# A pipelined Mamba block on one core: the order of the state sums, a one-tick shift of the post-processing, and the W2 additions on ScalarE and GpSimd

## The chip, the cores and the metric

The kernel runs on one core of one Trainium2 chip. The metric is device time in microseconds of one execution, as the median of several runs. The engines are named by short names: PE is TensorE (matmuls; PEld its weight loads), DVE is VectorE, ACT is ScalarE, POOL is GpSimd, SP is SyncE, which issues nearly all DMAs.

## The reference, cut to what matters

The input is x of shape (4, 1024, 256), float32, and all arithmetic is float32.

```
x = x + block(layernorm(x))
x = x + (fwht(silu(n @ W1.T) * (n @ W3.T))) @ W2.T      # n = layernorm(x), hidden 1024

block(h):                       # h is (4, 1024, 256)
  z, xs, B, C, raw = split(rmsnorm(h) @ in_proj.T)       # 256, 64, 64, 256, 128 columns
  dt = softplus(raw @ dt_proj.T + bias)                  # 256 channels, 32 states each
  for each time step:  s = exp(dt * A) * s + dt * xs * B ;  y = sum over states of s * C
  h = h + ((y + xs * D) * silu(z)) @ out_proj.T
  h = h + (silu(r @ gate.T) * (r @ up.T)) @ down.T       # r = rmsnorm(h), hidden 704
```

The recurrence over 1024 time steps has 256 channels x 32 states per batch element. The Hadamard transform (fwht) is folded into W2 at the start, into the tile `w2h`.

## The kernel before, in words

**Units and ticks.** The work is cut into 8 units: 4 batch elements times 2 halves of 512 time steps (`c` is 0 or 1; a unit with c = 1 starts from states that the unit before kept in `carry`). A unit's scan is 16 steps q, each with 4 tiles `da` of 128 x 512: 128 rows are 4 channels times 32 states, 512 columns are time. A step takes two ticks of the program, with two of the four tiles in each, so a unit's scan is 32 ticks, and E = 32k + 31 is the last tick of unit k.

**What a tick of the scan does.** ACT makes two exponentials (line 725) for the step after the present one, that is two ticks ahead. DVE makes one product `bx` of two tiles (line 749; it reads `ub` from a DMA and `pb`, the copy of B in PSUM that ACT makes once for eight steps, line 738) and two scans (line 759). POOL then multiplies two tiles of the tick before by C (line 777), keeps their last column in `carry` for c = 0 (line 776), or multiplies the first column of the next tick's tiles by it for c = 1 (`start_from`, line 766, which the next scans wait for). In every even tick PE sums the states of the step before with four matmuls (`sum_states`, line 791), each from one tile to 32 rows of one PSUM tile `py`. Tiles 0 and 1 are multiplied in the tick before, tiles 2 and 3 in the same tick. The sums free the `da` tile, of which there are 4, for a DMA three steps ahead. After eight steps DVE adds x * D (`y_dx`, line 806) one tick after the last sum and POOL multiplies by silu(z) (`y_z`, line 811) one tick after that.

**What runs around it.** The steps of `pre(u, H)` prepare unit u, whose scan begins at tick H: row statistics, `un`, transposes, the projections x and dt's input (`pe_x`, `act_x`), dt (`pe_dt`), C (`pe_c`). The steps of `post(u, E, other)` follow its scan, beside the scan of the next units: the out projection wo and its addition to `hr` (from E+3), row statistics, `small2` (rsqrt, on POOL), `hn`, its transposes and their copies `ht`, the gated product of the 704 hidden columns in two groups of three chunks (`gated`: gate projections pg on PE, then up projections pu, silu of pg on ACT, copies of pu on ACT, the product on POOL), `wd` and its addition, row statistics, `small3`, `hn`, transposes, the gated product with W1 and W3 in groups of 3, 3 and 2 chunks, then W2 with its addition from E+36 and the store at E+43. The last is at the time of the next unit's E+4 and after, so that one unit's W2 follows the next unit's wo on PE. `gated` also takes in the z projections of the unit after next (`other`), if there is one.

**What sets the order.** The order is written by hand. `at(tick, lane, fn)` puts a step on a tick and a lane. The main loop at the end (lines 853 to 891) runs over the ticks, and in each runs the lanes in a fixed order: PE, ACT, the `bx` product, ACTb (`pb` alone), two exponentials, first scan, the DVE lane, second scan, POOL0, the multiplication by C, `start_from`, POOL, the sums, PEend, ACTend, SP, the scan's DMAs, SPend. Steps of one lane and tick stand in the order in which they were put there: those of all `pre` first, then those of `post` from the earliest unit on. Every engine works off its instructions in the order of the program, so an engine that waits for one step holds up all behind it. `copy_b` (`pb`) is on the last lane but one before the exponentials, in the tick before each eighth step, that is at E+16 and E+32 of a unit's post-processing.

**PSUM and copies.** All matmuls but the sums write to `dense`, a ring of four PSUM tiles of 128 x 512; a new one waits until the one four before has been read. The copies `up` use a ring of three tiles in SBUF.

In `add_rows` (line 296) each of the four row tiles t takes one matmul per chunk, two row tiles share a PSUM tile, and DVE adds that to `hr` with one instruction of 128 x 512 (line 316) one tick after the second.

Of the kernel before, what the change touches and what calls it, by code (L numbers as in the profile page):

```python
# [9 lines left out]
F32 = mybir.dt.float32  # L10
AF = mybir.ActivationFunctionType
ALU = mybir.AluOpType
# [3 lines left out]
P = 128  # L16
# [3 lines left out]
T = 512  # L20
TT = T // P
# [6 lines left out]
def tile_block(ctx: ExitStack, tc: tile.TileContext, a, out):  # L28
# [20 lines left out]
    nc = tc.nc  # L49
# [112 lines left out]
    def row_stats(u, src, ts, centred=True):  # L162

        if 0 in ts:
            u["mv"] = sm.tile([P, 2, TT], F32, tag="mv", name="mv")
        for t in ts:
            junk = p1.tile([P, DM], F32, tag="junk", name="junk")
            nm, ms = u["mv"][:, 0, t : t + 1], u["mv"][:, 1, t : t + 1]
            if centred:
                nc.scalar.activation(  # L170
                    junk, src[:, t, :], AF.Identity, scale=-1.0 / (16 * DM), accum_out=nm
                )
            nc.scalar.activation(
                junk,
                src[:, t, :],
                AF.Square,
                bias=nm if centred else 0.0,
                scale=1.0 / 16,
                accum_out=ms,
            )  # L180
# [27 lines left out]
    def transposes(u, src):  # L208

        u["pt"] = [dense_psum() for _ in range(2)]  # L210
        for k in range(2):
            for t in range(TT):
                nc.tensor.transpose(  # L213
                    u["pt"][k][:, t * P : (t + 1) * P], src[:, t, k * P : (k + 1) * P], ident
                )
# [22 lines left out]
    def at(tick, lane, fn, *args):  # L238
        todo[tick][lane].append(partial(fn, *args))
# [5 lines left out]
    def gated(tick, u, dst, wa, wb, chunks, src, z=None):  # L245


        g = [{} for _ in chunks]
        pe_z, act_z = z[0]["z"] if z else (None, None)

        def pe(i, name, w):
            c, n = chunks[i]
            if n < P:

                both = project(W[w], c * P, 2 * n, u[src])
                g[i]["pg"], g[i]["pu"] = both, both[n:]
            else:
                g[i][name] = project(W[w], c * P, n, u[src])

        def silus():  # L260
            for i, (_, n) in enumerate(chunks):
                g[i]["si"] = p3.tile([P, T], F32, tag="si", name="si")
                nc.scalar.activation(g[i]["si"][:n], g[i]["pg"][:n], AF.Silu)  # L263
            if z:
                act_z(z[1])

        def up(i):
            n = chunks[i][1]
            g[i]["up"] = p3.tile([P, T], F32, tag="up", name="up")
            nc.scalar.copy(g[i]["up"][:n], g[i]["pu"][:n])  # L270

        def product(i):
            c, n = chunks[i]
            nc.gpsimd.tensor_tensor(u[dst][:n, c, :], g[i]["si"][:n], g[i]["up"][:n], ALU.mult)  # L274

        three = len(chunks) == 3
        steps = [(i, *s) for s in (("pg", wa), ("pu", wb)) for i in range(len(chunks))]
        steps = [s for s in steps if chunks[s[0]][1] == P or s[1] == "pg"]
        late = z and len(steps) == 6
        steps = [(pe, *s) for s in steps]  # L280
        if z:
            steps.insert(3, (pe_z, z[1]))
        for k, step in enumerate(steps):
            at(tick + k // 2, "PE", *step)
        at(tick + 1, "ACTend" if three else "ACT", silus)
        at(tick + 2, "ACT", up, 0)
        for i in range(1, len(chunks)):
            if i == 2 and late:
                at(tick + 3, "ACT", up, i)
            else:  # L290
                at(tick + 2, "ACTend", up, i)
        at(tick + 2, "POOL", product, 0)
        for i in range(1, len(chunks)):
            at(tick + 3, "POOL", product, i)

    def add_rows(tick, u, lhs, rhs, per_tick, lane="PE"):

        po = {}

        def pe(t):  # L300
            if t % 2 == 0:
                po[t // 2] = dense_psum().rearrange("p (t d) -> p t d", t=2)
            left, right = lhs(), rhs()
            n = len(left)
            for k in range(n):
                nc.tensor.matmul(  # L306
                    po[t // 2][:, t % 2, :],
                    lhsT=left[k][:, t * P : (t + 1) * P],
                    rhs=right[k],
                    start=(k == 0),  # L310
                    stop=(k == n - 1),
                )

        def add(i):
            hr = u["hr"][:, 2 * i : 2 * i + 2, :]
            nc.vector.tensor_tensor(hr, hr, po[i], ALU.add)  # L316

        for t in range(TT):
            at(tick + t // per_tick, lane, pe, t)
            if t % 2:  # L320
                at(tick + t // per_tick + 1, "DVE", add, t // 2)


    def pre(u, H):

        s = {}
# [217 lines left out]
        if H == 32:  # L544

            at(0, "ACTend", lambda: row_stats(u, u["x"], (0, 1)))
            at(1, "ACTend", lambda: row_stats(u, u["x"], (2, 3)))
            at(3, "POOL", small)
            at(5, "POOL", small_end)
            at(4, "ACT", un, (0, 1))  # L550
            at(5, "ACT", un, (2, 3))
            at(6, "PE", lambda: transposes(u, s["un"]))
            at(6, "ACTend", transposed, u, "ut")
        else:
            at(H - 54, "SP", load_x, u)
            at(H - 45, "ACTend", lambda: row_stats(u, u["x"], (0, 1)))
            at(H - 43, "ACTend", lambda: row_stats(u, u["x"], (2, 3)))
            at(H - 39, "POOL", small)
            at(H - 37, "POOL", small_end)
            at(H - 32, "ACT", un, (0, 1))  # L560
            at(H - 31, "ACT", un, (2, 3))
            at(H - 30, "PE", lambda: transposes(u, s["un"]))
            at(H - 30, "ACTend", transposed, u, "ut")
        at(H - 25, "PE", pe_x)
        at(H - 24, "ACT", act_x)
        at(H - 23, "SP", dma_xb)
        at(H - 19, "SPend", dma_xr, 0)
        at(H - 17, "SPend", dma_xr, 1)
        at(H - 16, "PE", pe_dt)
        at(H - 16, "PE", pe_c, 0)  # L570
        if H == 32:
            for h in range(2):
                at(H - 11, "PE", pe_z, h)
# [16 lines left out]
    def post(u, E, other):  # L590


        s = {}
# [41 lines left out]
            4,  # L635
            "PEend",
        )
        at(E + 5, "ACTend", lambda: row_stats(u, u["hr"], (0, 1), False))
        at(E + 6, "ACTend", lambda: row_stats(u, u["hr"], (2, 3), False))
        at(E + 7, "POOL", small2)  # L640
        at(E + 8, "ACT", hn, "r3", None)
        at(E + 9, "PE", lambda: transposes(u, s["tok"]))
        at(E + 9, "ACTend", transposed, u, "ht")
        at(E + 9, "POOL", lambda: nc.gpsimd.tensor_tensor(u["hr"], u["hr"], u["x"], ALU.add))
        at(E + 10, "PE", big, "m")
        sizes = [min(P, DFF - c * P) for c in range(6)]
        chunks = list(enumerate(sizes))
        for i in range(2):
            gated(E + 10 + 3 * i, u, "m", "wg", "wu", chunks[3 * i : 3 * i + 3], "ht",
                  (other, i) if other else None)  # L650
        add_rows(
            E + 18,
            u,
            lambda: [u["m"][:n, c, :] for c, n in enumerate(sizes)],
            lambda: [W["wd"][:n, c, :] for c, n in enumerate(sizes)],
            1,
        )
        at(E + 20, "ACTend", lambda: row_stats(u, u["hr"], (0, 1)))
        at(E + 22, "ACTend", lambda: row_stats(u, u["hr"], (2, 3)))
        at(E + 23, "POOL", small3)  # L660
        at(E + 24, "ACT", hn, "r4", "nm")
        at(E + 25, "PE", lambda: transposes(u, s["tok"]))
        at(E + 25, "ACTend", transposed, u, "xt")
        at(E + 26, "PE", big, "g")
        chunks8 = [(c, P) for c in range(8)]
        for i in range(3):
            gated(E + 26 + 3 * i, u, "g", "w1", "w3", chunks8[3 * i : 3 * i + 3], "xt")
        add_rows(
            E + 36,
            u,  # L670
            lambda: [u["g"][:, c, :] for c in range(8)],
            lambda: [w2h[:, c, :] for c in range(8)],
            1,
        )
        at(E + 43, "SPend", store)

# [107 lines left out]
    def sum_states(q):  # L784
        s = qs[q]
        u = s["u"]
        first, last = s["n"] % 8 == 0, s["n"] % 8 == 7
        if first:
            u["py"] = ps_y.tile([P, T], F32, tag="y", name="py")
        for b in range(4):  # L790
            nc.tensor.matmul(  # L791
                u["py"][32 * b : 32 * b + 32, :],
                lhsT=rsel[:, 2 * s["j"] + s["g"], :],
                rhs=s["da"][:, b, :],
                start=first,
                stop=last,
            )
        if last:
            at(2 * q + 3, "DVE", y_dx, u, s["h"])
            at(2 * q + 4, "POOL0", y_z, u, s["h"])  # L800
# [159 lines left out]
```

## Time and profile before

| | |
|---|---|
| median of 3 runs | 1186.88 us (1186.69 to 1189.98) |
| the profiled execution | 1190.86 us, span of its instructions 1189.1 us |
| granted TensorE clock, mean | 0.903 |
| PE busy | 1023.6 us, 86% of the span |
| DVE busy | 961.1 us, 81% |
| POOL busy | 903.0 us, 76% |
| ACT busy | 773.8 us, 65% |
| two scans (line 759), mean of one | 1210 ns, 512 of them |
| multiplication by C (line 777) | 2358 ns, 256 of them |
| product of silu and up (line 274) | 1272 ns, 64 with W1 and W3, 48 of the first gated product |
| addition to `hr` on DVE (line 316) | 675 ns, 48 of them |
| copy of a PSUM tile on ACT (line 270) | 578 ns |

A timeline row gives the start and the length in us, the engine, the line, the operation, the tiles written and read, how many instructions were merged, and in brackets the idle time of the engine before it with what ended it. A matmul of float32 leaves two records on PE, so "x8" at line 791 is the four sums of one step. Lengths of neighbouring instructions of an engine overlap a little, so the cost of one that stands between others is read from start to start.

### The profile page before, as it was taken

To read this page: it belongs to the slowest core of one execution; us is meant where nothing else is said; L and a number is where in the kernel's file an instruction comes from. 1 tells how busy PE (TensorE), PEld (TensorE's weight loads), DVE (VectorE), ACT (ScalarE), POOL (GpSimd) and SP (SyncE) were. 2 spreads that over 40 slices of the span, in tenths; PEclk is the share of its full clock that TensorE was granted. 3 is DMA by queue.
4 is the path that set the end of the run, shared out by engine and by line. 5 is a ranking of instruction groups with operands and counts; after the bars stand their busy time and mean duration, and the time that the engine had idled before them with its cause. 6 is when DMAs were issued, how large, how long until landed. Compare 5 with 4: busy or idle time off the path is not lost.

```text
span 1189.1 us, 12244 instructions
## 1 busy us (share of the span) xinstructions
PE 1023.6 (86%) x3374; PEld 471.1 (40%) x3374; DVE 961.1 (81%) x860; ACT 773.8 (65%) x1391; POOL 903.0 (76%) x807
## 2 busy tenths in 40 slices
PE   8475467989998989988998989988998989699988
PEld 3121022433633355433634354433634353336535
DVE  4797889899889979899889979898989989992000
ACT  3746564878478775879478767878576847573331
POOL 6675768879788978889788978889787978784212
PEclk9776668989898889989998989988998989889989
DMA  7989998898699879888799869998689869840000
GB/s 246 336 308 355 358 338 296 310 329 284 238 337 306 327 244 313 318 327 296 252 339 313 302 225 342 313 335 282 242 315 322 308 243 328 307 155 1 18 0 18
DMA packets 89444, 321.91 MB, mean 271 GB/s; under 512 B 9312, under 2 KB 20000, under 8 KB 73120
## 3 DMA queue, kind: packets, MB, share of 16 engines
q1 hardware_dynamic: 87520, 318.38, 75.7%
q10 hardware_dynamic: 1856, 2.75, 0.6%
q8 instruction: 27, 0.44, 0.1%
q14 instruction: 41, 0.34, 0.1%
HBM read 302.22 MB, written 18.87 MB: 270 GB/s over the span
## 4 chain that ended last, share of the span: by engine, by line
PE 44%; POOL 16%; DVE 10%; issue 8%; DMA 4%; ACT 4%; SPq 0%; DVEq 0%; POOLq 0%; ACTq 0%
PE dense L226 23%; PE dense L306 14%; POOL da L777 10%; PE py L791 6%; DVE da L759 5%; DVE bx L749 4%; POOL g L274 3%; ACT da L725 1%; DMA ub<-ud 1%; DMA cd<-cc 1%; POOL m L274 1%; DVE hr L316 1%; PE dense L213 1%; DMA xr<-xbd 1%; POOL yt L811 1%
## 5 line engine op out<-in xcount | busy, mean ns | idle before, releaser
L777 POOL TENSOR_TENSOR da<-da,cr 128x1024 f32<-128x1024 f32 x256 | 603.7, 2358 | 100.1 <-DVE da L759 52.2
L759 DVE TENSOR_TENSOR_SCAN da<-da,bx 128x512 f32<-128x512 f32 x512 | 602.0, 1210 | 43.7 <-ACT da L725 10.4
L725 ACT ACTIVATE da<-da,nega 128x512 f32<-128x512 f32 x508 | 331.4, 713 | 68.8 <-DMA da<-dtd 65.4
L791 PE MATMUL py<-da,rsel 128*32 128x512 f32 x1024 | 226.7, 685 | 134.7 <-POOL da L777 132.8
L749 DVE TENSOR_TENSOR bx<-ub,pb 128x1024 f32<-128x1024 f32 x254 | 312.1, 1229 | 30.5 <-ACT pb L738 19.2
L226 PE MATMUL dense<-xt,w 128*128 128x512 f32 x512 | 228.8, 601 | 0.0
L226 PEld LDWEIGHTS dense<-xt,w 128*128 128x128 f32 x512 | 95.6, 191 | 136.0 <-issue 111.8
L791 PEld LDWEIGHTS py<-da,rsel 128*32 128x32 f32 x1024 | 29.9, 113 | 270.7 <-POOL da L777 213.8
L316 DVE TENSOR_TENSOR hr<-hr,dense 128x512 f32<-128x512 f32 x48 | 32.4, 675 | 127.6 <-PE dense L306 127.6
L306 PE MATMUL dense<-w2h,g 128*128 128x256 f32 x512 | 113.4, 380 | 0.0
L306 PE MATMUL dense<-wd,m 128*128 128x256 f32 (+1 forms) x384 | 103.6, 417 | 0.9 <-POOL m L274 0.9
L306 PEld LDWEIGHTS dense<-w2h,g 128*128 128x128 f32 x512 | 96.8, 190 | 18.4 <-issue 5.5
L270 ACT COPY up<-dense 128x512 f32<-128x512 f32 x112 | 63.4, 578 | 58.3 <-PE dense L226 58.1
L274 POOL TENSOR_TENSOR g<-si,up 128x512 f32<-128x512 f32 x64 | 80.8, 1272 | 25.8 <-ACT up L270 25.4
L226 PE MATMUL dense<-ut,win 128*128 128x512 f32 x192 | 94.1, 623 | 0.2 <-ACT ut L220 0.2
L274 POOL TENSOR_TENSOR m<-si,up 128x512 f32<-128x512 f32 (+1 forms) x48 | 60.4, 1273 | 41.3 <-ACT up L270 41.3
L226 PE MATMUL dense<-ht,wg 128*128 128x512 f32 x192 | 89.4, 610 | 2.6 <-ACT ht L220 2.6
L263 ACT ACTIVATE si<-dense 128x512 f32<-128x512 f32 x112 | 63.0, 596 | 39.7 <-PE dense L226 38.1
L306 PEld LDWEIGHTS dense<-wd,m 128*128 128x128 f32 (+1 forms) x384 | 72.3, 201 | 40.0 <-issue 24.0
L200 ACT ACTIVATE hn<-hr,s 128x256 f32<-128x256 f32 x64 | 30.3, 543 | 88.9 <-POOL s L196 74.8
L226 PE MATMUL dense<-ht,wu 128*128 128x512 f32 x160 | 72.2, 597 | 0.0
L776 POOL COPY carry<-da 128x2 f32<-128x2 f32 x128 | 23.8, 186 | 61.5 <-DVE da L759 59.5
(92 smaller groups left out, 798.5 us busy)
## 6 DMA issues: line engine op xcount, KB each, us to landing
da<-dtd SPq DMA_DIRECT2D x127, 1024.0 KB
ub<-ud SPq DMA_DIRECT2D x254, 512.0 KB
cr<-cd SPq DMA_DIRECT2D x64, 256.0 KB
x<-in_x SPq DMA_DIRECT2D x8, 512.0 KB
dtd<-dt SPq DMA_DIRECT2D x16, 256.0 KB
ud<-du SPq DMA_DIRECT2D x16, 256.0 KB
cd<-cc SPq DMA_DIRECT2D x16, 256.0 KB
out<-hr SPq DMA_DIRECT2D x8, 512.0 KB
```

Of the source, the lines that this page charges most:

```text
L200: nc.scalar.activation(dst[:, t, :], src[:, t, :], AF.Identity, bias=bias[:, t : t + 1] if bias is not None else 0.0, scale=scale[:, t : t ...
L226: nc.tensor.matmul(dst[:n], lhsT=w[:, k, col : col + n], rhs=src[:, k, :], start=(k == 0), stop=(k == 1),)
L263: nc.scalar.activation(g[i]["si"][:n], g[i]["pg"][:n], AF.Silu)
L270: nc.scalar.copy(g[i]["up"][:n], g[i]["pu"][:n])
L274: nc.gpsimd.tensor_tensor(u[dst][:n, c, :], g[i]["si"][:n], g[i]["up"][:n], ALU.mult)
L306: nc.tensor.matmul(po[t // 2][:, t % 2, :], lhsT=left[k][:, t * P : (t + 1) * P], rhs=right[k], start=(k == 0), stop=(k == n - 1),)
L316: nc.vector.tensor_tensor(hr, hr, po[i], ALU.add)
L725: nc.scalar.activation(da, da if q else s["u"]["pdt", b], AF.Exp, scale=an[:, s["h"], s["j"], b, s["g"] : s["g"] + 1],)
L749: nc.vector.tensor_tensor(s["bx"], s["ub", b0 // 2], u["pb"].unsqueeze(1).broadcast_to([P, 2, T]), ALU.mult)
L759: nc.vector.tensor_tensor_scan(da, da, s["bx"][:, b % 2, :], start, ALU.mult, ALU.add)
L777: nc.gpsimd.tensor_tensor(s["da"][:, two, :], s["da"][:, two, :], s["cr"].unsqueeze(1).broadcast_to([P, 2, T]), ALU.mult,)
L791: nc.tensor.matmul(u["py"][32 * b : 32 * b + 32, :], lhsT=rsel[:, 2 * s["j"] + s["g"], :], rhs=s["da"][:, b, :], start=first, stop=last,)
```

## The change

The states of a step are summed beginning with tiles 2 and 3. In the post-processing the row statistics of the four row tiles behind wo are taken in one tick, and all steps from there to the gated product with W1 and W3 stand one tick earlier; W2 and the store stay. The silu of every group is on the lane ACTend (for groups of two chunks it was on ACT). In the preparation `un` and its transposes, `pe_dt` and the first `pe_c` stand one tick earlier; `x = max(H - 25, 7)` gives the same tick as before for every unit. The additions behind W2 are made in two steps, but for the last unit: ACT copies the PSUM tile to SBUF, and POOL adds the copy to `hr` a tick later.

```diff
-        three = len(chunks) == 3
         steps = [(i, *s) for s in (("pg", wa), ("pu", wb)) for i in range(len(chunks))]
...
-        at(tick + 1, "ACTend" if three else "ACT", silus)
+        at(tick + 1, "ACTend", silus)
...
-    def add_rows(tick, u, lhs, rhs, per_tick, lane="PE"):
+    def add_rows(tick, u, lhs, rhs, per_tick, lane="PE", on_pool=False):
...
+        def evict(i):
+            ev = p3.tile([P, T], F32, tag="up", name="ev")
+            po[i] = ev.rearrange("p (t d) -> p t d", t=2), po[i]
+            nc.scalar.copy(*po[i])
+
+        def add_pool(i):
+            hr = u["hr"][:, 2 * i : 2 * i + 2, :]
+            nc.gpsimd.tensor_tensor(hr, hr, po[i][0], ALU.add)
+
         for t in range(TT):
             at(tick + t // per_tick, lane, pe, t)
             if t % 2:
-                at(tick + t // per_tick + 1, "DVE", add, t // 2)
+                after = tick + t // per_tick + 1
+                if on_pool:
+                    at(after, "ACTend", evict, t // 2)
+                    at(after + 1, "POOL", add_pool, t // 2)
+                else:
+                    at(after, "DVE", add, t // 2)
...
-            at(H - 32, "ACT", un, (0, 1))
-            at(H - 31, "ACT", un, (2, 3))
-            at(H - 30, "PE", lambda: transposes(u, s["un"]))
-            at(H - 30, "ACTend", transposed, u, "ut")
-        at(H - 25, "PE", pe_x)
-        at(H - 24, "ACT", act_x)
-        at(H - 23, "SP", dma_xb)
+            at(H - 33, "ACT", un, (0, 1))
+            at(H - 32, "ACT", un, (2, 3))
+            at(H - 31, "PE", lambda: transposes(u, s["un"]))
+            at(H - 31, "ACTend", transposed, u, "ut")
+        x = max(H - 25, 7)
+        at(x, "PE", pe_x)
+        at(x + 1, "ACT", act_x)
+        at(x + 2, "SP", dma_xb)
...
-        at(H - 16, "PE", pe_dt)
-        at(H - 16, "PE", pe_c, 0)
+        at(H - 17, "PE", pe_dt)
+        at(H - 17, "PE", pe_c, 0)
...
-        at(E + 5, "ACTend", lambda: row_stats(u, u["hr"], (0, 1), False))
-        at(E + 6, "ACTend", lambda: row_stats(u, u["hr"], (2, 3), False))
-        at(E + 7, "POOL", small2)
-        at(E + 8, "ACT", hn, "r3", None)
-        at(E + 9, "PE", lambda: transposes(u, s["tok"]))
-        at(E + 9, "ACTend", transposed, u, "ht")
-        at(E + 9, "POOL", lambda: nc.gpsimd.tensor_tensor(u["hr"], u["hr"], u["x"], ALU.add))
-        at(E + 10, "PE", big, "m")
+        at(E + 5, "ACTend", lambda: row_stats(u, u["hr"], range(TT), False))
+        at(E + 6, "POOL", small2)
+        at(E + 7, "ACT", hn, "r3", None)
+        at(E + 8, "PE", lambda: transposes(u, s["tok"]))
+        at(E + 8, "ACTend", transposed, u, "ht")
+        at(E + 8, "POOL", lambda: nc.gpsimd.tensor_tensor(u["hr"], u["hr"], u["x"], ALU.add))
+        at(E + 9, "PE", big, "m")
...
-            gated(E + 10 + 3 * i, u, "m", "wg", "wu", chunks[3 * i : 3 * i + 3], "ht",
+            gated(E + 9 + 3 * i, u, "m", "wg", "wu", chunks[3 * i : 3 * i + 3], "ht",
...
         add_rows(
-            E + 18,
+            E + 17,
...
-        at(E + 20, "ACTend", lambda: row_stats(u, u["hr"], (0, 1)))
-        at(E + 22, "ACTend", lambda: row_stats(u, u["hr"], (2, 3)))
-        at(E + 23, "POOL", small3)
-        at(E + 24, "ACT", hn, "r4", "nm")
-        at(E + 25, "PE", lambda: transposes(u, s["tok"]))
-        at(E + 25, "ACTend", transposed, u, "xt")
-        at(E + 26, "PE", big, "g")
+        at(E + 19, "ACTend", lambda: row_stats(u, u["hr"], (0, 1)))
+        at(E + 21, "ACTend", lambda: row_stats(u, u["hr"], (2, 3)))
+        at(E + 22, "POOL", small3)
+        at(E + 23, "ACT", hn, "r4", "nm")
+        at(E + 24, "PE", lambda: transposes(u, s["tok"]))
+        at(E + 24, "ACTend", transposed, u, "xt")
+        at(E + 25, "PE", big, "g")
...
-            gated(E + 26 + 3 * i, u, "g", "w1", "w3", chunks8[3 * i : 3 * i + 3], "xt")
+            gated(E + 25 + 3 * i, u, "g", "w1", "w3", chunks8[3 * i : 3 * i + 3], "xt")
         add_rows(
             E + 36,
...
             1,
+            on_pool=u is not us[-1],
...
-        for b in range(4):
+
+        for b in (2, 3, 0, 1):
```

## The prediction

> **What bounds the kernel now.** I read the page's busy shares first, then the waits of VectorE (DVE) one by one in the timeline, and then followed each of the two large ones back through TensorE (PE), ScalarE (ACT) and GpSimd (POOL). The unit whose post-processing begins near 563 us stands for units 1 to 5, whose rows repeat every 132 us. E is the last tick of a unit's scan; "s at E+3" means the sums over states at that tick, and pg, pu are gate and up products by chunk.
>
> ```profile
> PE 1023.6 (86%) x3374; PEld 471.1 (40%) x3374; DVE 961.1 (81%) x860; ACT 773.8 (65%) x1391; POOL 903.0 (76%) x807
> ```
>
> No engine is full, so the bound changes hands within a unit. DVE's own waits in one unit:
>
> ```profile
> 568.05 0.69 DVE L316 TENSOR_TENSOR hr<-hr,dense 128x512 f32<-128x512 f32 x1 [2.71 <-PE dense L306]
> 569.78 0.69 DVE L316 TENSOR_TENSOR hr<-hr,dense 128x512 f32<-128x512 f32 x1 [1.04 <-PE dense L306]
> 577.73 0.66 DVE L316 TENSOR_TENSOR hr<-hr,dense 128x512 f32<-128x512 f32 x1
> 619.86 1.23 DVE L749 TENSOR_TENSOR bx<-ub,pb 128x1024 f32<-128x1024 f32 x1 [2.46 <-ACT pb L738]
> ```
>
> The waiting additions are those behind wo (E+4). The additions behind W2, the ones that the change moves, are at 577.73 and 585.71 and wait for nothing. The next wait is for pb, the copy of B that ACT makes at E+16. ACT before it, and PE before that:
>
> ```profile
> 615.03 0.58 ACT L270 COPY up<-dense 128x512 f32<-128x512 f32 x1 [1.18 <-PE dense L226]
> 615.63 1.28 ACT L725 ACT_TABLE_LOAD   x1
> 616.93 1.33 ACT L725 ACTIVATE da<-da,nega 128x512 f32<-128x512 f32 x2
> 618.17 1.17 ACT L270 COPY up<-dense 128x512 f32<-128x512 f32 x2
> 619.24 0.58 ACT L738 COPY pb<-br 128x512 f32<-128x512 f32 x1
> ```
> ```profile
> 563.32 1.86 PE L791 MATMUL py<-da,rsel 128*32 128x512 f32 x4 [3.92 <-POOL da L777]
> ...
> 590.11 1.19 PE L791 MATMUL py<-da,rsel 128*32 128x512 f32 x8
> 591.69 5.42 PE L226 MATMUL dense<-ht,wg 128*128 128x512 f32 x12 [0.39 <-ACT ht L220]
> ...
> 613.06 3.60 PE L226 MATMUL dense<-ht,wu 128*128 128x512 f32 x8
> ```
>
> From 563.32 PE runs to 622 with one idle gap of 0.39 us, and ACT's copies wait for it. So from s at E+3 to the up projection of chunk 3 (half of the last row: 614.9) PE is the bound, 51.6 us; ACT then takes 4.9 us to pb. From 619.9 to 691.2 DVE is the bound, 71.3 us. The last piece is POOL's:
>
> ```profile
> 662.95 0.18 POOL L776 COPY carry<-da 128x2 f32<-128x2 f32 x1 [0.23 <-DVE da L759]
> ...
> 690.61 1.28 POOL L274 TENSOR_TENSOR g<-si,up 128x512 f32<-128x512 f32 x1
> 691.84 1.28 POOL L811 TENSOR_TENSOR yt<-yt,zs 128x512 f32<-128x512 f32 x1
> 693.06 2.36 POOL L777 TENSOR_TENSOR da<-da,cr 128x1024 f32<-128x1024 f32 x1
> 695.52 1.27 POOL L274 TENSOR_TENSOR g<-si,up 128x512 f32<-128x512 f32 x1
> ```
>
> POOL has no gap after 662.95, and its product at 693.06 lets the next s at E+3 start: 4.3 us more. 51.6+4.9+71.3+4.3 = 132.1 us, the period. A change in this loop costs or gains in full; elsewhere it is hidden.
>
> **W2's additions.** Two of 0.58 us (577.73 to the scan at 578.31) leave DVE in each of seven units. They lie between wo's addition and the pb multiply, where DVE already waits 2.46 us: the wait becomes 3.6 and nothing is gained. Only unit 6, whose rows show no pb wait, gains 1.2 us. In return ACT gets two copies of 0.58 us and POOL two additions; the nearest row is the product of that size, 1.27 us. They fall at E+6 to E+9. ACT stands idle 10.4 us there (the wait of hn for the row scale), and POOL idles 4.6 and 1.4 us, so I cost them at 0; were that cover gone, 1.2 and 2.5 us per unit. [...]
>
> **Order of the sums.** Four sums behind one wait take 1.06 us (584.61, eight records), two take 1.05 (621.21, four records): each writes 32 rows of its own. So waiting for the last-multiplied tiles first costs nothing at the end, and it spares up to 1.05 us only where PE is late and the wait still splits them. Inside the stretch that bounds they are together already: 0. PE's wait before s at E+3 gets longer, since the earlier pair no longer runs inside it; the two now go at half clock (1.86), and four should take no more than that, with 0 to 1.9 us as bounds. [...]
>
> **One tick earlier, on PE.** The transposes of hn now go right behind pe_x, and s at E+9 no longer stands between them and the gate product. That sum covered ACT's copies of ht (1.19 us of cover and 0.39 idle). The copies and the copy of xb (which frees a PSUM tile) still end near 591.6, so pg starts where it did, and the sum comes after it: +1.06 us, up to chunk 3 with no other change in the list of matmuls. Five units: +5.3.
>
> **On ACT.** pu of chunks 3 to 5 are copied at E+14 instead of E+15, but pb stays at E+16. So the exponentials of E+15 now stand between the copies and pb, and those of E+14, which had run before the silu, stand behind the first copy. ACT cannot start that copy sooner, for PE is the bound. The path from pu to pb grows from 4.9 by one pair of exponentials, 1.3 us. Five units: +6.5. If PE were a tick ahead this would cost 0.
>
> **On POOL.** Products of m are queued one tick earlier too, at E+11, +12, +14, +15, and still wait for the up copies. Behind the waiting product stand the multiplications by C. In the rows of before POOL waits 1.06 and 1.82 us for "up"; now m of chunk 3 stands before the multiplication of E+15, and chunks 4 and 5 before that of E+16. The carry starts (L766) behind it feed the scans of c=1, and y_dx at E+18 waits for the sums behind it. By hand the multiplication of E+17 ends 4 us later than 624.5; DVE itself is 2.4 us later by the two terms above, which leaves 0 to 2.6 us. I take the middle, 1.3; five units: +6.5.
>
> At the other end g's last product moves from behind the multiplication of E+3 (695.52) to before it, and POOL has no gap since 662.95 to take it up, save 0.23: 1.27-0.23 = +1.04. It counts seven times: +7.3. With a gap it would cost 0.
>
> **Other moves, at 0.** un, its transposes, dt and the first C product go a tick earlier where PE or ACT idle (PE waits 3.9 us before E+3; 2.33 at 624.59, where a quarter of wd now runs). No DMA is moved; loads of da on SP follow the sums that free their tiles, and a sum at E+15 later by up to 4 us eats into a lead of six ticks, 22 us. wd's additions at E+19 and E+21 have about a tick less ahead of them: 0 to 1 us, taken 0. Merging the row statistics only shortens the way to hn, for which PE does not wait there. The end, after 1081, is a chain of matmuls in the same order: 0.
>
> **Sum.** 5.3+6.5+6.5+7.3-1.2 = +24.4 us. The profiled execution took 1190.9 us (span 1189.1), 4.0 over the median of the runs: 1215.3 on its scale, 1211 on theirs. With the two middling terms at their ends (POOL's at 0 or 2.6, the clock at 0 or 1.9 in six units): 1205 to 1229.
>
> **Rivals.** (1) Faster: DVE is the bound after all. Its place is the stretch from wo's addition to pb, its price 14 x 0.58 = 8 us, and 5 x 2.5 = 12 more if pb no longer waits: 1167 to 1179, say 1173. It decides if PE has pu of chunk 3 done 4.8 us sooner than 614.9, for DVE would want pb at 616.2 and ACT's path is now 6.2. For it: the steps are a tick (3.7 us) earlier, and PE idles more before E+3. Against it: PE's start at E+3 hangs on POOL, and its 51.6 us are full. (2) No change: PE and ACT slip as said, but the earlier silus give ACT enough lead that pb is not late, and POOL finds a gap: 1187. (3) Worse: POOL's blocked multiplications count in full and the clock is low for longer in E+3 to E+7: 24.4+6.5+11.4 = +42, 1229. (4) The reordered sums do not run side by side at half clock; that is the 1.9 us in (3).
>
> **How the numbers follow.** The forecast, 1205 to 1218, has 0.52; rival 3, up to 1232, 0.17; rival 2, 0.08; rival 1, 0.23. This measurement tells 0.3% (3.6 us) from no change: faster 0.23, same 0.07, slower 0.70. The range from 1172 to 1228 leaves out about half of rival 1 and a third of rival 3, under 0.2 in all; the slower cases alone span 1200 to 1232.
>
> **What would show it.** Right: DVE's pb wait grows from 2.46 to about 6 us in units 1 to 5, with an exponential pair between the last up copy and pb; PE still has no gap from E+3 to chunk 3; the sum of E+9 stands behind two gate products; POOL idles before m of chunk 3 with multiplications queued behind. Wrong: the pb wait shrinks or goes, the period falls below 131 us, or POOL shows gaps before g's last product.

## The result, and the profile after

The changed kernel takes 1215.92 us (median, 1214.83 to 1217.11) and the kernel before, timed beside it, 1187.64 us (1186.69 to 1189.98). The ratio is 1.0235 with an interval of 1.0216 to 1.0254: 28 us slower, where 24 were predicted. The profiled execution took 1214.83 us, its span is 1213.0 us, and the mean granted clock of PE is 0.891 (0.903 before).

The busy shares again show no full engine. PE's busy time has fallen because sums that stood alone now run side by side (the sums take 167.0 us in place of 226.7):

```profile
PE 973.1 (80%) x3374; PEld 465.9 (38%) x3374; DVE 952.3 (79%) x846; ACT 786.4 (65%) x1407; POOL 918.4 (76%) x821
```

The quickest account of a change of span is one engine's idle time, by the group that waited and what released it. Here are DVE's two largest groups, scans and bx, of the kernel before first and then of the changed one. The columns are count, busy time and mean, then the idle time before the group and its main releasers.

```profile
L759 DVE TENSOR_TENSOR_SCAN da<-da,bx 128x512 f32<-128x512 f32 x512 | 602.0, 1210 | 43.7 <-ACT da L725 10.4 <-POOL da L766 6.3 <-DVE bx L749 4.2
L749 DVE TENSOR_TENSOR bx<-ub,pb 128x1024 f32<-128x1024 f32 x254 | 312.1, 1229 | 30.5 <-ACT pb L738 19.2 <-DMA ub<-ud 2.5
```
```profile
L773 DVE TENSOR_TENSOR_SCAN da<-da,bx 128x512 f32<-128x512 f32 x512 | 600.6, 1209 | 79.1 <-POOL da L780 31.1 <-ACT da L739 20.6 <-DVE bx L763 3.2
L763 DVE TENSOR_TENSOR bx<-ub,pb 128x1024 f32<-128x1024 f32 x254 | 312.2, 1229 | 18.3 <-ACT pb L752 7.9 <-DMA ub<-ud 1.6
```

The scans wait 35.4 us more, for carry starts (POOL, 6.3 to 31.1) and exponentials (ACT, 10.4 to 20.6). bx waits 12.2 less. Of the smaller groups y_dx waits 7.2 more and the additions to hr 2.4 more, and DVE has 8.8 us less to do. That makes 24.0 of the 23.9 us by which the span grew. The wait for pb, which the prediction wanted to grow, fell from 19.2 to 7.9.

Take the unit whose post-processing begins at 575.6 us, beside a scan with c = 0. Behind wo's additions DVE's main waits are these: the scans of E+15, pb at E+16, y_dx at E+18 and a carry start near the end:

```profile
630.67 2.33 DVE L773 TENSOR_TENSOR_SCAN da<-da,bx 128x512 f32<-128x512 f32 x2 [3.34 <-ACT da L739]
634.07 1.23 DVE L763 TENSOR_TENSOR bx<-ub,pb 128x1024 f32<-128x1024 f32 x1 [1.07 <-ACT pb L752]
...
644.05 0.75 DVE L821 SCALAR_TENSOR_TENSOR yt<-xr,dpar,py 128x512 f32<-128x512 f32 x1 [3.64 <-PE py L806]
...
702.90 2.33 DVE L773 TENSOR_TENSOR_SCAN da<-da,bx 128x512 f32<-128x512 f32 x2 [2.18 <-POOL da L780]
```

ACT there, from the up copy of chunk 3 to pb:

```profile
628.01 0.59 ACT L270 COPY up<-dense 128x512 f32<-128x512 f32 x1 [2.37 <-PE dense L226]
...
629.91 1.33 ACT L739 ACTIVATE da<-da,nega 128x512 f32<-128x512 f32 x2
631.15 1.17 ACT L270 COPY up<-dense 128x512 f32<-128x512 f32 x2
632.22 1.33 ACT L739 ACTIVATE da<-da,nega 128x512 f32<-128x512 f32 x2
633.46 0.57 ACT L752 COPY pb<-br 128x512 f32<-128x512 f32 x1
```

The pair of exponentials predicted between the last up copy and pb is there (632.22). The earlier pair stands behind the first copy, and DVE waits for that one first (3.34 us), then for pb (1.07). Together that is 4.41 us where the kernel before waits 2.46 and the prediction said about 6. The path goes on as predicted, but most of the wait shows under another name.

PE has no gap over 0.24 us from E+3 to chunk 3, and the sums of E+9 (607.10) stand behind two gate products:

```profile
575.60 1.94 PE L806 MATMUL py<-da,rsel 128*32 128x512 f32 x8 [6.73 <-POOL da L791]
...
603.47 3.70 PE L226 MATMUL dense<-ht,wg 128*128 128x512 f32 x8 [0.24 <-ACT ht L220]
607.10 1.07 PE L806 MATMUL py<-da,rsel 128*32 128x512 f32 x8
...
625.94 3.70 PE L226 MATMUL dense<-ht,wu 128*128 128x512 f32 x8
632.56 1.94 PE L806 MATMUL py<-da,rsel 128*32 128x512 f32 x8 [2.92 <-POOL da L791]
```

Chunk 3 is done at 627.8, 52.2 us after the start of E+3 (51.6 before). From there to bx at 634.07 it is 6.27 us (4.96 before). And from bx to the next E+3 at 714.1 it is 80.0 us (75.6 before), of which y_dx's wait is 3.64. This is one of the longer units: from one wo to the next it takes 138.5 us and its neighbours 134.6, where in the kernel before every unit but the last takes 131 to 133. In the unit that follows, beside a scan with c = 1, DVE has none of these waits for exponentials, pb and y_dx; there it waits five times for carry starts, 1.27 to 2.41 us each. In the unit shown POOL works without a gap from 673.4 us up to the multiplication of E+3, with g's last product now ahead of it:

```profile
709.23 1.27 POOL L274 TENSOR_TENSOR g<-si,up 128x512 f32<-128x512 f32 x1
...
711.68 2.35 POOL L791 TENSOR_TENSOR da<-da,cr 128x1024 f32<-128x1024 f32 x1
```

At 575.60 and 632.56 the sums run at a granted clock of 0.50 (four in 1.94 us, where four at 607.10 take 1.07).

### The profile page after: what moved, and what is told of

Its sections match the earlier page's. It is cut to its first block, busy times and chain, and to the rows that moved or that the text cites. A ratio compares the mean times of both kernels' runs of the same rounds, so it can differ in the third digit from the quotient of the medians.

```text
span 1213.0 us, 12214 instructions
## 1 busy us (share of the span) xinstructions
PE 973.1 (80%) x3374; PEld 465.9 (38%) x3374; DVE 952.3 (79%) x846; ACT 786.4 (65%) x1407; POOL 918.4 (76%) x821
## 5 line engine op out<-in xcount | busy, mean ns | idle before, releaser
L773 DVE TENSOR_TENSOR_SCAN da<-da,bx 128x512 f32<-128x512 f32 x512 | 600.6, 1209 | 79.1 <-POOL da L780 31.1
L806 PE MATMUL py<-da,rsel 128*32 128x512 f32 x1024 | 167.0, 730 | 216.7 <-POOL da L791 216.7
L763 DVE TENSOR_TENSOR bx<-ub,pb 128x1024 f32<-128x1024 f32 x254 | 312.2, 1229 | 18.3 <-ACT pb L752 7.9
L226 PE MATMUL dense<-xt,w 128*128 128x512 f32 x512 | 232.9, 607 | 0.1
L806 PEld LDWEIGHTS py<-da,rsel 128*32 128x32 f32 x1024 | 21.5, 115 | 306.2 <-POOL da L791 272.1
L315 DVE TENSOR_TENSOR hr<-hr,dense 128x512 f32<-128x512 f32 x34 | 23.0, 676 | 130.0 <-PE dense L305 130.0
L226 PE MATMUL dense<-ut,win 128*128 128x512 f32 x192 | 105.5, 686 | 0.2 <-ACT ut L220 0.2
L274 POOL TENSOR_TENSOR g<-si,up 128x512 f32<-128x512 f32 x64 | 80.9, 1274 | 24.3 <-ACT up L270 23.9
L305 PE MATMUL dense<-wd,m 128*128 128x256 f32 (+1 forms) x384 | 97.1, 396 | 0.9 <-POOL m L274 0.9
L305 PEld LDWEIGHTS dense<-wd,m 128*128 128x128 f32 (+1 forms) x384 | 68.5, 190 | 38.7 <-issue 28.5
L226 PEld LDWEIGHTS dense<-ut,win 128*128 128x128 f32 x192 | 41.2, 223 | 68.8 <-issue 53.4
L790 POOL COPY carry<-da 128x2 f32<-128x2 f32 x128 | 23.9, 187 | 54.5 <-DVE da L773 52.4
```

What stands on the lines that cost most here:

```text
L226: nc.tensor.matmul(dst[:n], lhsT=w[:, k, col : col + n], rhs=src[:, k, :], start=(k == 0), stop=(k == 1),)
L305: nc.tensor.matmul(po[t // 2][:, t % 2, :], lhsT=left[k][:, t * P : (t + 1) * P], rhs=right[k], start=(k == 0), stop=(k == n - 1),)
L763: nc.vector.tensor_tensor(s["bx"], s["ub", b0 // 2], u["pb"].unsqueeze(1).broadcast_to([P, 2, T]), ALU.mult)
L773: nc.vector.tensor_tensor_scan(da, da, s["bx"][:, b % 2, :], start, ALU.mult, ALU.add)
L790: nc.gpsimd.tensor_copy(carry_of(s)[:, two], s["da"][:, two, T - 1])
L806: nc.tensor.matmul(u["py"][32 * b : 32 * b + 32, :], lhsT=rsel[:, 2 * s["j"] + s["g"], :], rhs=s["da"][:, b, :], start=first, stop=last,)
```

## Experiments

Every kernel was timed beside the kernel before. Ratios are to that kernel, and differences are between the medians of one comparison.

### The three parts alone, and all but the shift

The first holds only the tick shift of `post` and of the silus, the second only the order of the sums, the third only W2's additions. The fourth is the changed kernel with the shift of `post` and the silu lane taken back.

```diff
 only_sums, the kernel before with:
-        for b in range(4):
+        for b in (2, 3, 0, 1):
 only_w2, the kernel before with:
+            on_pool=u is not us[-1],
```

> The kernel before with the post-processing's shift alone. Theory: about the whole loss, 1210 to 1219 us, with the waits of the changed kernel: exponentials 3.3 and y_dx 3.7 us in units beside a scan with c = 0, carry starts of 1.3 to 2.4 us four times beside one with c = 1. Rival (W2 additions or sums cost the time): 1187 to 1195 us.

> The kernel before with the order of the sums alone (tiles 2, 3, 0, 1). Theory: no difference, 1185 to 1189 us: in the stretch from E+3 to chunk 3 the four sums run side by side already; the sum at E+3 takes 1.9 us as before, with a longer wait ahead of it (about 5 instead of 3.9 us). Rival (the longer idle time closes the clock for longer, up to 1.9 us in six units): 1190 to 1199 us.

> The kernel before with the additions behind W2 copied by ScalarE and made by GpSimd, alone. Theory: VectorE's 1.2 us in each unit turn into a longer wait for pb (2.5 to about 3.7 us), only unit 6 gains: 1185 to 1188 us. Rival (GpSimd's 2.5 us more in each unit lie on the path): 1195 to 1205 us. If VectorE were the bound there: 1179 us.

> The changed kernel with all steps of the post-processing put back on their ticks of before; the order of the sums, the additions behind W2 on ScalarE and GpSimd, and the earlier un, dt and first C product stay. Theory (the shift of the gated product blocks ScalarE and GpSimd behind a TensorE that is not ahead): the loss goes, 1185 to 1189 us, waits of VectorE as before (about 2.5 for pb and 3.7 + 1.0 for wo in each unit). Rival (the W2 additions or the reordered sums cost the time, through GpSimd's 2.5 us more in each unit and TensorE's longer idle time before E+3): 1205 to 1216 us.

| kernel | us, median | ratio, 95% | over before |
|---|---|---|---|
| the shift alone | 1206.07 | 1.0140 (1.0126 to 1.0154) | 16.6 |
| the order of the sums alone | 1198.79 | 1.0083 (1.0069 to 1.0096) | 9.3 |
| W2's additions alone | 1188.21 | 0.9995 (0.9984 to 1.0006) | -1.3 |
| all but the shift | 1198.50 | 1.0079 (1.0063 to 1.0095) | 9.0 |

The parts add up to 24.6 of 28.3 us. The shift costs less than the 25.6 us that its terms had, and less than expected before its run. The order of the sums, put at 0, costs a third of the whole; the expectations of no loss, for it and for the fourth kernel, both missed by that much. The fourth kernel, which also holds the preparation's steps a tick earlier, stands at the sum of the last two parts within 1 us (9.0 against 8.0), so those steps cost nothing that shows. W2's additions cost nothing that the interval shows, and the row says why. With them alone, DVE's wait for pb in that unit is

```profile
617.63 1.23 DVE L764 TENSOR_TENSOR bx<-ub,pb 128x1024 f32<-128x1024 f32 x1 [3.59 <-ACT pb L753]
```

The two additions of 0.58 us went, and the wait grew from 2.46 to 3.59 us.

### What the order of the sums costs: the clock

In the kernel with the order alone PE waits 4.84 us at E+3, 3.63 at E+23 and 1.96 at E+25. Of PE from E+23 on, before and then with the new order:

```profile
643.05 1.05 PE L791 MATMUL py<-da,rsel 128*32 128x512 f32 x4
647.04 1.05 PE L791 MATMUL py<-da,rsel 128*32 128x512 f32 x4 [2.94 <-POOL da L777]
...
652.38 3.65 PE L791 MATMUL py<-da,rsel 128*32 128x512 f32 x8
655.97 7.13 PE L226 MATMUL dense<-xt,w 128*128 128x512 f32 x16
```
```profile
647.85 1.93 PE L806 MATMUL py<-da,rsel 128*32 128x512 f32 x8 [3.63 <-POOL da L791]
...
655.24 1.93 PE L806 MATMUL py<-da,rsel 128*32 128x512 f32 x8 [1.96 <-POOL da L791]
657.10 8.77 PE L226 MATMUL dense<-xt,w 128*128 128x512 f32 x16
```

Before, the pair from tiles 0 and 1 ran at 643.05, at the head of the wait, and the next four took 3.65 us at 652.38, as two pairs at half clock would (1.86 each). With all four behind one wait PE stands still longer (3.63, 0.68 and 1.96 us from E+23 to W1, where it was 2.94 and 1.56), and the first sixteen matmuls with W1 take 8.77 us in place of 7.13. The granted clock in these stretches (windows by engine; the third number from the end is the clock), before and with the new order:

```profile
647.00:655.90 8.90, 7.13 (x20) 1.99 (x20) 8.60 (x8) 6.99 (x13) 7.13 (x10) 0.62 1.01 364
655.90:663.00 7.10, 7.10 (x18) 2.96 (x16) 6.70 (x7) 4.19 (x6) 6.39 (x8) 1.00 0.87 322
```
```profile
647.80:657.10 9.30, 6.55 (x25) 1.88 (x25) 9.01 (x8) 7.00 (x13) 7.51 (x10) 0.50 0.98 353
657.10:665.80 8.70, 8.70 (x21) 3.61 (x17) 8.19 (x8) 4.30 (x6) 7.92 (x9) 0.81 0.90 340
```

The clock stays at half for 13.7 us here where it did for 6.8, and the sum of such times over the span is 287 us against 230. By the record of the granted clock the half-clock stretches at E+23 add up to 68.3 us in units 1 to 5, where they were 41.0; those at E+3 add up to 37.6 us in six units with either order. DVE shows how this becomes time: y_dx of a scan's second half waits for sums that stand on PE behind the products with W3. Its row, before and with the new order:

```profile
L806 DVE SCALAR_TENSOR_TENSOR yt<-xr,dpar,py 128x512 f32<-128x512 f32 x16 | 11.7, 733 | 7.5 <-PE py L791 7.2
```
```profile
L821 DVE SCALAR_TENSOR_TENSOR yt<-xr,dpar,py 128x512 f32<-128x512 f32 x16 | 11.8, 737 | 16.0 <-PE py L806 16.0
```

That is 8.5 us more, where scans, bx and the additions to hr together wait 3.0 less and the span grew by 7.0.

To test whether the clock is the cause, two kernels put a pair of matmuls with zero weights where the early pair had run. The first does so ahead of all sums, the second only where PE waits (E+3, E+23, E+25).

```diff
+        waits = s["n"] in (0, 10, 11)              # the second; the first: every step
+        for b in (0, 1) if waits else ():
+            nc.tensor.matmul(u["py"][32 * b : 32 * b + 32, :], lhsT=zero, rhs=s["da"][:, b, :], start=first, stop=False)
         for b in (2, 3, 0, 1):
...
-                start=first,
+                start=first and (b > 1 or not waits),
```

> The kernel before with the order 2, 3, 0, 1 of the sums (1198.8 us alone), and two more matmuls with a weight of zeros ahead of each four, on the tiles b = 0 and 1; they add nothing to the sums, but they run where the earlier pair ran in the kernel before, inside PE's wait for the second multiplication by C. If the 9.4 us are the clock, which closes for longer once nothing runs inside that wait (288 us at half clock against 231), they come back: 1187 to 1191, half-clock time near 231, and the windows at E+23 to E+26 shrink from 13.7 to about 6.8 us. If it is the order itself (all four sums behind the last multiplication, which delays what PE has behind them), the time stays at 1197 to 1201, and the two matmuls may add a little.

> As the kernel with a pair of zero-weight matmuls ahead of every four sums (1218 us), but with that pair only ahead of the sums of E+3, E+23 and E+25, where PE waits and the earlier pair had run in the kernel before; where PE does not wait the extra pair cost about 0.9 us each, which is what the other kernel's 1218 us should be. If the 9.4 us of the order 2, 3, 0, 1 are a clock that stays closed for longer, they now come back: 1187 to 1192, and the half-clock windows at E+23 shrink from 13.7 to 6.8 us. If it is the order itself, 1197 to 1201, though the windows shrink.

The first takes 1217.97 us (1.0237, 1.0204 to 1.0270), which neither theory had expected. Its trace says why. Where PE does not wait, the two extra matmuls cost it about 0.85 us a step (from the pair's start at 598.55 to the next matmul at 600.39 it is 1.84 us, where the four sums alone take 1.0): the zero pair goes to the rows of the real pair, and the six don't all run side by side. There are five such steps from E+3 to chunk 3, in the stretch that bounds, and DVE's wait for pb there grows to 6.11 us. The half-clock time did fall, to 172 us, but the kernel couldn't answer the question. The second one does: 1188.01 us, ratio 0.9986 (0.9973 to 1.0000), with half-clock time at 226 us and y_dx's wait at 7.4. The stretch reads as before:

```profile
643.90:653.00 9.10, 7.35 (x29) 2.04 (x29) 8.80 (x8) 6.98 (x13) 7.33 (x10) 0.62 0.96 348
653.00:660.00 7.00, 7.00 (x20) 2.95 (x16) 6.60 (x7) 3.84 (x6) 6.28 (x8) 1.00 0.90 345
```

The order 2, 3, 0, 1 is still in this kernel, so the order itself costs nothing. Its 9.3 us are the clock's. The three places were given the pair together; that E+23 and E+25 are the ones that matter rests on the clock's record, not on a run.

### The terms of the shift

Each of these is the kernel with the shift alone, with one kind of step put back to its old tick: the products of m on POOL; the products of g on POOL; the products of m and the up copies of m on ACT.

```diff
 in gated(), dp and du are 1 for the group named and 0 else:
-        at(tick + 2, "ACT", up, 0)
+        at(tick + 2 + du, "ACT", up, 0)
...
-        at(tick + 2, "POOL", product, 0)
+        at(tick + 2 + dp, "POOL", product, 0)
```

> The kernel before with the post-processing a tick earlier (1206.1 us alone, 16.6 over before), but with the products of m on POOL at the ticks that they had before, so that no product stands ahead of the multiplications by C that were ahead of it. The POOL term of the prediction, 6.5 us (bounds 0 to 13): 1193 to 1206, likeliest 1199.5, and the waits of DVE's scans for the carry starts (1.3 to 2.3 us each in the second halves of a sequence) go. If the products' place on POOL is not what costs, the time stays at 1205 to 1207 and the waits only change their releaser.

> The kernel before with the post-processing a tick earlier (1206.1 us), but with the products of g on POOL at the ticks that they had before, so that the last one is again behind the multiplication of E+3. By the prediction's term, 1.04 us in seven units: 1198 to 1200. If POOL has a gap there after all, or the next wait takes its place: 1205 to 1207.

> As the kernel with m's products at the ticks they had before, and m's up copies on ACT at theirs too, so that the exponentials stand around them as before and only the silus and the matmuls of m are a tick earlier. If the ACT term of the prediction holds (6.5 us for one pair of exponentials between the copies and pb in five units), it lies 5 to 7 us below the kernel with the products alone; what is then left over before is the PE term and the product of g, 5 and 7 us, so 1199 or less, down to 1194. If the copies' place costs nothing (the exponentials that went behind them wait in any case), the two kernels are equal within 1.5 us.

| the shift with | us, median | ratio, 95% | over before |
|---|---|---|---|
| products of m put back | 1200.30 | 1.0106 (1.0065 to 1.0146) | 11.8 |
| products of g put back | 1202.92 | 1.0114 (1.0085 to 1.0143) | 14.4 |
| products and up copies of m put back | 1188.49 | 0.9996 (0.9978 to 1.0013) | 0.0 |

Against the 16.6 us of the shift, the products of m return 4.8 us and those of g 2.2 (6 to 8 were expected); the intervals of both overlap that of the shift alone, so neither is clear of the noise. The scans' wait for carry starts was expected to go with the products of m and went only from 30.9 to 25.3 us. The up copies of m return another 11.8 us, which is clear of the noise and more than the theory's 5 to 7. ACT in the last kernel, with pu of chunk 3 done at 611.2:

```profile
610.32 1.33 ACT L739 ACTIVATE da<-da,nega 128x512 f32<-128x512 f32 x2
611.56 0.56 ACT L271 COPY up<-dense 128x512 f32<-128x512 f32 x1
...
614.34 0.58 ACT L752 COPY pb<-br 128x512 f32<-128x512 f32 x1
```

The table load (609.02, 1.28 us) and the exponentials of E+14 (610.32) now run while PE makes chunk 3, where in the changed kernel they stand behind a copy that waits 2.37 us for PE. From pu to bx it takes 3.8 us, against 6.27 in the changed kernel and 4.96 before.

### A better version

If the early products and copies are the loss, a shift without them should gain. These kernels put back m's up copies and all products. The second also has W2's additions on ACT and POOL, and the third was also to copy m's last chunk behind pb instead of ahead of it. The sums keep their old order.

```diff
+        dp, du = 1, int(dst == "m")
...
 the third:
-                at(tick + 3 + du, "ACT", up, i)
+                at(tick + 3 + du, "ACTc", up, i)    # ACTc runs behind ACTb, the lane of pb
```

> The kernel before with the post-processing a tick earlier, but m's up copies and all products of m and g at the ticks they had before: only matmuls, silus, row statistics and g's up copies are earlier. By addition of the two runs: 1188.5 less 3.1 for g's products, 1185.4 (1183 to 1187). If the wait for g's carry starts (2 to 2.4 us at E+32 in shift_mup) is replaced by a wait of PE's at E+3: 1188.

> The same with W2's additions copied by ScalarE and made by GpSimd. They save DVE 2 x 0.58 us in seven units, between wo's addition and pb, where DVE's wait for pb is now 1.05 us instead of 2.46. By the prediction's loop (PE bounds that stretch) nothing is gained but 1.2 us in the last unit: 1184. If DVE bounds it once pb is early, up to 8 us: 1177 to 1180.

> The same once more, with the last up copy of m (chunk 5) on ACT right behind the copy of pb instead of right before it. If pb is what DVE waits for there, it comes 0.58 us earlier in each of five units: 2 to 3 us less than the kernel without. If DVE then waits for the exponentials or for the copy's product on POOL (0.58 us later), nothing or up to 3 us more.

They take 1182.69 us (0.9935, 0.9914 to 0.9956), 1181.93 us (0.9925, 0.9902 to 0.9947) and 1181.04 us (0.9930, 0.9906 to 0.9954): faster than the kernel before by 0.7% and than the changed one by some 3%, and no different from each other within their intervals. The first is 6.5 us under before, where the addition of the two runs had given 3.1. Nothing more came of W2's additions here than of W2's additions alone. The third kernel doesn't test what it was meant to: the changed line is reached only for a group of three full chunks, so it moves the copy of m's third chunk, in a tick without pb. The last chunk has 64 columns, and its copy stays. In the trace both copies (613.27 and 613.86) still stand ahead of pb (614.34), and DVE's wait for pb there is 1.55 us, as in the second. Whether a copy behind pb would gain stays open. In the first of the three, DVE's scans wait as follows, to be set against the groups of before and after above:

```profile
L773 DVE TENSOR_TENSOR_SCAN da<-da,bx 128x512 f32<-128x512 f32 x512 | 601.8, 1209 | 49.7 <-POOL da L780 14.1 <-ACT da L739 9.0 <-DVE bx L763 5.8
```

The carry starts are at 14.1 instead of 31.1 us and the exponentials at 9.0 instead of 20.6, while bx's wait for pb is 7.9 us, as low as in the changed kernel. Against the kernel before, the scans wait 6.0 us more, bx 12.2 less (18.3 for 30.5) and the additions to hr 2.2 less (125.4 for 127.6): 8.4 us less in all, where the span is 7.7 us shorter.

## Why the prediction was right in its total and wrong in its terms

The sign, the size and the place were right: the loop of PE, ACT, DVE and POOL does set the period, and most of the steps that were moved are on it. But that 24.4 us came out near 28 was partly luck, because errors cancelled: the order of the sums and part of the price of m's copies were missed, and two terms of the shift were too large.

**Order of the sums: put at 0, measured 9.3 us.** This is the step that failed. The prediction took the row of E+3, where the pair runs at half clock before (1.86 us), for every place where the sums wait, and put the longer wait ahead of them at 0. At E+3 the clock's record bears that out: 37.6 us at half clock with either order. Elsewhere it does not. From E+23 to E+25 PE has little but the sums and eight transposes to do; with the early pairs behind the waits the half-clock time there grows from 6.8 or 10.2 us to 13.7, and in the unit shown PE reaches the end of W3 1.7 us later, counted from the start of E+3 (689.98 less 563.97 against 687.65 less 563.32). In that unit 13.7 us at half clock go with the wait of 3.63 us at E+23, 6.8 with that of 2.94. The range took the clock at 0 or 1.9 us in six units, 11.4 in all, and rival 3 put these 11.4 at E+3 to E+7. No run shows that term: the runs show no more half-clock time at E+3, 27.3 us more of it at E+23 (68.3 less 41.0), and 9.3 us for the order. So rival 3's clock was near in size, though not in place. The runs also show that a pair of matmuls of 1 us at the head of a wait is enough to make that difference here: with the zero pair at three places the ratio to the kernel before is 0.9986, without it 1.0083.

**One tick earlier, on PE: put at +5.3, measured about 0.** The prediction had the gate product start where it did, with the sums of E+9 to pay behind it. But before, ACT's copies of ht stood behind the copy of raw and a pair of exponentials; in the changed kernel they are ahead of the copies of xb and raw. In the kernel with the shift alone the gate product starts 26.95 us after the start of E+3, not 28.37, and chunk 3 is done after 51.3 us (51.6 before, 52.2 in the changed kernel). The cover that was lost hid a wait that went too.

**On ACT: +1.3 us a unit, as predicted on that path.** From pu to bx it is 6.27 us in place of 4.96. Its price is more than the 6.5 us counted: putting the copies back returned 11.8. The term had looked at one path in units of c = 0. The same copies, when they wait for PE, also hold up POOL's products (m of chunk 3 waits 3.02 us for up with the shift alone, 2.73 with the products put back, 1.77 with the copies put back) and with them the carry starts of c = 1. And with the shift but the old copies the path is shorter than before (3.8 us against 4.96). How the 11.8 divide between these was not measured.

**On POOL: taken 6.5, measured 4.8** for the products of m, which is not clear of the noise; part of it is in the carry starts, as said (30.9 us with the shift alone, 25.3 with the products put back). **g's last product: put at 7.3, measured 2.2** alone, within the noise. The product does stand ahead of the multiplication of E+3. Once m's steps are back in place, putting back g's products (the step from 1188.5 to 1182.7) is worth about 6 us, clear of the noise. That the larger loss had hidden it is likely and not shown.

**W2's additions: right.** -1.2 us was said, a ratio of 0.9995 measured, whose interval (0.9984 to 1.0006) includes both that and no change, and the pb wait grew to 3.59 where 3.6 was written. The POOL additions took 1.27 us each, as the nearest row had said, where one on DVE takes 675 ns. That price decides nothing here, because neither side is on the path.

**The sign to look for was half wrong.** PE has no gap, the sums of E+9 stand behind two gate products, and POOL waits 3.03 us before m of chunk 3 (1.82 before), all as said. But the wait for pb did not grow to 6 us; it fell. The waits for exponentials and carry starts just ahead of it took its time, so a reader who looked only at the named row would have called the prediction refuted.

Of the rivals, the one that had DVE as the bound fell: taking additions off DVE moved nothing. The sums do run side by side at half clock (four in 1.94 us, where two take 1.86), so that rival fell too. The parts alone add to 24.6 us and the whole costs 28.3. In the changed kernel y_dx waits 3.64 to 3.68 us at E+18 of three units, in the unit shown behind sums and dt at half clock (0.50 from 631.8 to 638.6); with the shift alone these waits are 0.84 to 0.86, and with the order alone at most 0.25. That is where the two parts meet; no run separates its price.

## What to carry to other kernels

Before work is taken out of an engine's wait, ask what that work did for the engine's clock: PE's spare pair of sums cost nothing here, and the clock was at half for 6.8 or 10.2 us at E+23 with it and for 13.7 without. When a chain is moved a tick earlier, move its producers and leave the consumers that wait (here m's copies and all products) where they were, since what stands behind a waiting instruction waits too (in the changed kernel the exponentials of E+14, behind a copy that waits 2.37 us for PE); here leaving them there turned a loss of 16.6 us into a gain of 6.5. And read a predicted wait as a place, not as a row: DVE's waits for pb, exponentials and carry starts took over from each other.

## What the runs showed of the hardware

By the record of the granted clock in the kernel before and in the changed one, every half-clock stretch but the last of each lasted 3.4 us or a multiple of it: 28 before, of 3.4 to 20.5 us, and 33 in the changed kernel, of 3.4 to 37.5 us. The stretch from E+23 was 6.8 or 10.2 us in the kernel before and 13.7 us in each of units 1 to 5 with the new order of the sums alone. Zero weights keep the clock up as well as others here: with the pair of zeros at three places the time at half clock was 226 us, against 230 before. Sums that go to different 32 rows run side by side (four take 1.06 us, two 1.05, in the kernel before); with a zero pair to the rows of two of them, the six take 1.84 us.
